# GpSimd's factors behind attention's last sums, the fifth product bank by bank, and residual additions on GpSimd

## The chip, the cores and the metric

The kernel runs on one core of a Trainium2 chip. The metric is the device time of one launch in microseconds (us). The kernel before took 3298.68 us in the median of three runs (3296.69 to 3300.23).

## What is computed

Eight images, each of 512 channels by 1024 pixels in fp32, pass through two attention layers. Both layers have the same form and differ in their weights and in the size of the groups of the normalisation (8 and 32 groups):

```python
xn  = groupnorm(x) * gamma + beta                 # [512, 1024] per image
qkv = qkv_w @ xn + qkv_b                          # q, k, v: [512, 1024] each
# 8 heads of 64 channels
attn = softmax(q_h.T @ k_h / 8, axis=-1)          # [1024, 1024] per head
out_h = v_h @ attn.T
x = proj_w @ out + proj_b + x
```

## The kernel before, in words

**Units.** A unit is one image in one layer, and the 16 units run one after the other: 8 of layer 0, then 8 of layer 1. The order of the instructions on each engine is the order of the Python calls; there is no scheduler. What a later step waits for comes from semaphores that the framework places by tiles. Tile pools give a buffer to a new tile when its last user has done with it. The pool that matters here, `ppool`, has five buffers of 128x1024. It holds the exponentials `p`, the tiles `xa` and `xb` for factors, `oa` and `ob`, `u3_v`, and the residual tiles `res00`, `res01`, `res10`, `res11`.

**Fast products.** Every 512x512 by 512x1024 product is done with seven products of half size instead of eight (Strassen in Winograd's form), in the order 1, 6, 2, 7, 5, 4, 3 (`ORDER`). For V one such level is used, and for Q, K and the output projection two levels: each of the seven is again seven products of 128-row quarters (`Stream.product`, L421). The factors of the right-hand side are sums and differences of parts of `xn` (the normalised input) or `ao` (attention's result). `Right.mix` (L217) makes the outer ones on VectorE. `Right.quarter` makes the quarters: on GpSimd for `xn` (the lambda at L933 issues them), on VectorE for `ao` (L990). Three of a pair's four quarter steps need only the outer factors; the fourth overwrites its input in place, and must wait until TensorE has read it.

**Stages of a unit.** First come the value products (`make_values`, L398): seven of 16 matmul instructions, into three pairs of PSUM banks. Their results are taken out by ScalarE (L606, L621) and VectorE (L607, L625 for the sixth, L632 for the seventh). Then come Q and K (`make_pairs`), then the output projection of the unit before (`project`), then attention of this unit. `hook(sel, k)` runs further work behind product k of a stage; the lists are written out with `at(...)` in the main loop.

**A product of the stream** (`Stream.product`). The part products 1, 6 and 5 are summed one after the other in a spare half bank `one`. ScalarE copies (`seed`, L426) that running sum into the four quarters of the main pair of banks, where TensorE adds the other parts. A seed must wait until VectorE has read what stood in that bank two products earlier. The last two parts and the reading out (`tail`) of a product come behind the first part of the next one (`close`), so that the seeds are covered. The tail of the very last product comes behind the first scores of attention (`close()` in `scores`). One part product (7) goes out on its own as `late` (L438), and GpSimd adds it to the right half of the result (`add_late`, L458).

**Reading out.** In `sum_steps`, the running sums p1, u2 and u3 are made by VectorE (L466/L469, L478, L486). The fifth product is needed twice: `w` (L496) adds it to u2 over both banks, then L509 (Q, K) or L546 (output) adds it to a result over both banks.

**Residuals.** In `project`, `load` brings the four residual tiles from memory. `take` (L546) adds a product to a tile, `more` (L550, VectorE) adds a running sum, and `store` (L553) sends it to memory from SP's queue. The stores of res11, res10 and res01 come behind `more`.

**Attention.** 64 steps of scores (L703), exponential (ScalarE, L713) and products with V (L733). VectorE sums the exponentials (L750 for the first two of eight, then L752), which is the softmax's denominator. At the end of each eight steps come ScalarE's L758 and VectorE's L759 to take the result out, a transpose (L764) and a reduction (L772). `reciprocals` (L789 to L798) and `divide` (L812) follow later, for the last pair of heads in the next unit's value stage. TensorE runs the products two steps behind the scores at a unit's start.

**Weights.** The left-hand factors are mixed once per layer on VectorE (L1064 runs such steps), and stored in memory as images that later units load. `MAKE` says which unit's attention mixes which weights. In layer 0, V, Q and K are mixed in the first unit's value, Q and K stages, and the output weights in the first unit's attention.

Of the kernel before, what the change touches and what calls it, by code (L numbers as in the profile page):

```python
# [32 lines left out]
def fast_path(ctx, tc, x, qkv_wT, proj_wT, vecs, groups, out, flag):  # L33
# [5 lines left out]
    nc = tc.nc  # L39
# [4 lines left out]
    FD = 512  # L44
# [415 lines left out]
    def sum_steps(l, bias, name, early=None):  # L460
# [32 lines left out]

        def w(main, m):
            t = st["u2"]
            on("DVE", nc.vector.tensor_add(t, main, t), m, 0, 1)  # L496

        return st, p1, u2, u3, w

    def make_pairs(stream, w, sel, bias, left, early, hook):  # L500
# [13 lines left out]
        def fifth(main, m, late):  # L514
            wide(main, m)
            result(1, 1, "u3")(main, m, late)

# [14 lines left out]
    def project(stream, w, left, hook):  # L532
# [15 lines left out]

        def more(r, h, name):
            add(res[r, h], res[r, h], st[name])  # L550

# [11 lines left out]
        def fifth(main, m, late):  # L563
            wide(main, m)
            take(1, 1, main, m, late)

        def fourth(*args):
            take(1, 0, *args)
            more(1, 1, "u3")
            store(1, 1)  # L570

        def third(*args):
            take(0, 1, *args)
            more(1, 0, "u3")
            store(1, 0)
            more(0, 1, "u2")
            store(0, 1)
# [98 lines left out]

    def attention(w, close, at_step):
        u = w.u
# [5 lines left out]
        def scores(s):  # L684
# [16 lines left out]
            for j in range(2):  # L701
                for e in range(2):
# [6 lines left out]
                    )  # L709
            if s == 0:  # L710
                close()
            p = ppool.tile([P, 2, FD], F32, tag="p", name=f"p_{u}_{s}")
# [180 lines left out]
    }  # L893
    MAKE = {0: (0, "o"), 1: (1, "v"), 2: (1, "q"), 3: (1, "k"), 4: (1, "o")}

    old = None
    for u in range(2 * B):
# [36 lines left out]

        at("v", 1, make_rooms, partial(right.mix, 3), part_of((2, 3), 0, 1, 2))
        at("v", 6, part_of((5, 6), 0, 1, 2))
        at("v", 2, partial(right.mix, 2), part_of((1, 7), 0, 1, 2))
        at("v", 7, part_of((1, 7), 3), part_of((4,), 0, 1, 2))
        at("v", 5, part_of((5, 6), 3))
        at("v", 4, part_of((4,), 3))  # L940
# [5 lines left out]
        if u == 0:  # L946
# [24 lines left out]
            at("q", 4, partial(run, inner_k[2:3]))  # L971
            at("q", 3, partial(run, inner_k[3:]), partial(store_image, 0, "k", left_first_k))
        else:

# [3 lines left out]
            def o_rooms(first_rooms):  # L978
                if first_rooms:
                    ta, tb = (trpool.tile([P, 2, FD], F32, tag="tr", name=f"o{i}_{u}") for i in "ab")  # L980
                    oa = ppool.tile([P, 2, FD], F32, tag="p", name=f"oa_{u}")
                    rooms = {(1, 7): (*halves(ta), halves(tb)[0]), (5, 6): (halves(tb)[1], *halves(oa))}
                else:
                    ob = ppool.tile([P, 2, FD], F32, tag="p", name=f"ob_{u}")
                    rooms = {(2, 3): (*halves(ob), halves(xt[:, 0])[0]), (4,): singles(xt[:, 1])}
                for pair, room in rooms.items():
                    o_parts[pair] = ro.quarter(pair, room, nc.vector)
# [38 lines left out]
        if u:  # L1026
            product = project(stream, old, left_slots[1], hook)
            at("k", 4, partial(old.load_res, 0, 0))
            at("k", 3, partial(load_xn, ahead, 2), partial(old.load_res, 1, 1), partial(old.load_res, 1, 0))
            at("o", 1, partial(stats_of, 0, 1))  # L1030
            at("o", 2, partial(stats_of, 2))
            at("o", 7, partial(stats_of, 3, 4))
            at("o", 5, partial(old.load_res, 0, 1))
            at("o", 4, partial(stats_of, 5))
            at("o", 3, partial(stats_of, 6, 7))
        else:
            at("k", 3, partial(load_xn, ahead, 2))
# [52 lines left out]

        attention(w, stream.close, at_step)
        old = w
# [277 lines left out]
```

## Time and profile before

| | |
|---|---|
| median of 3 runs | 3298.68 us (3296.69 to 3300.23) |
| the profiled execution | 3297.93 us, span 3296.1 us |
| TensorE (PE) busy | 3221.7 us, 98% |
| weight loads (PEld) | 2083.2 us, 63% |
| VectorE (DVE) | 2900.7 us, 88% |
| ScalarE (ACT) | 1888.6 us, 57% |
| GpSimd (POOL) | 889.7 us, 27% |
| granted TensorE clock | 0.998 |
| one unit (1435.59 to 1638.33 us) | 202.74 us; TensorE busy 199.77, VectorE 180.78, GpSimd 56.40 |
| GpSimd's step of a 128x512 quarter | 1.27 us at the least, 2.0 to 2.2 us where VectorE works beside it |
| store of a residual tile, issue to landing | 2.7 us median |

A row of the timeline gives the start in the span, the duration, the engine, the source line, the instruction, the tiles written and read, and the number of merged instructions; in brackets is the idle time before it and what ended that. A row of waits gives the engine and line that waited, whom it waited for, the total, the number of times and the longest. `issue` means that the engine waited for nothing that the profile shows. TensorE's matmuls overlap each other, so its idle time is best read from the pitch between starts.

### The profile page before, as it was taken

Reading aid. Unit: us, or ns where it says so; the run is one execution under the profiler, and the core shown is the slowest. Engines: PE = TensorE matmul, PEld = TensorE weight load, DVE = VectorE, ACT = ScalarE, POOL = GpSimd, SP = SyncE. Lnnn points to the kernel's source line nnn. Section 1 sums busy time; section 2 is a strip of 40 time slices with the busy share of each in tenths; the row PEclk is TensorE's granted clock in tenths of the full one; section 3 lists DMA queues with packets and bytes.
Section 4 is the critical chain, followed back from the end, with each engine's and each line's share of the span. In section 5 each row is a group of like instructions: output and inputs, shape, how many; then the busy total and the mean of one; then the engine's idle time right before and its main releaser. Section 6 shows DMA issues by size and latency. Waiting matters only on the chain.

```text
span 3296.1 us, 59529 instructions
## 1 busy us (share of the span) xinstructions
PE 3221.7 (98%) x22998; PEld 2083.2 (63%) x22998; DVE 2900.7 (88%) x3298; ACT 1888.6 (57%) x3077; POOL 889.7 (27%) x559
## 2 busy tenths in 40 slices
PE   9999999999999999999999999999999999999999
PEld 7466584665856658566584765847657575675753
DVE  7998989889898898998989989898898988989887
ACT  3645746457464574646646466574655746557464
POOL 5033140330413304132140422404223042330510
PEclk9999999999999999999999999999999999999999
DMA  5234243442424324233142331423314233232321
GB/s 192 81 128 129 77 142 99 129 129 94 133 89 138 122 60 136 80 104 115 55 143 79 108 119 41 155 73 102 123 48 151 73 114 105 76 124 78 112 74 48
DMA packets 151343, 344.82 MB, mean 105 GB/s; under 512 B 27152, under 2 KB 40976, under 8 KB 151056
## 3 DMA queue, kind: packets, MB, share of 16 engines
q1 hardware_dynamic: 151056, 340.94, 32.5%
q8 instruction: 186, 3.05, 0.4%
q14 instruction: 101, 0.83, 0.1%
HBM read 282.29 MB, written 57.02 MB: 103 GB/s over the span
## 4 chain that ended last, share of the span: by engine, by line
PE 70%; DVE 21%; issue 5%; ACT 2%; DMA 1%; SPq 0%; POOL 0%; DVEq 0%; ACTq 0%
PE s L703 18%; PE a L733 17%; PE s L421 17%; PE a L421 12%; DVE acc L752 9%; PE s L398 2%; PE a L398 2%; DVE tr L764 2%; DVE acc L750 2%; DVE ao L759 1%; ACT p L713 1%; DMA lt<-red 1%; DVE red L772 1%; DVE tot L793 1%; PE a L703 1%
## 5 line engine op out<-in xcount | busy, mean ns | idle before, releaser
L713 ACT ACTIVATE p<-s 128x1024 f32<-128x1024 f32 x976 | 1000.3, 1025 | 528.1 <-PE s L703 446.5
L733 PE MATMUL a<-p,v 64*64 64x512 f32 x8192 | 1123.1, 590 | 8.6 <-ACT p L713 8.6
L703 PE MATMUL s<-q,k 64*64 64x512 f32 x7808 | 1083.4, 591 | 3.5 <-ACT a L426 2.6
L752 DVE TENSOR_TENSOR acc<-acc,p 128x1024 f32<-128x1024 f32 x768 | 995.6, 1296 | 55.0 <-ACT p L713 5.6
L733 PEld LDWEIGHTS a<-p,v 64*64 64x64 f32 x8192 | 410.2, 131 | 479.8 <-ACT p L713 336.8
L703 PEld LDWEIGHTS s<-q,k 64*64 64x64 f32 x7808 | 424.1, 133 | 392.1 <-issue 383.6
L426 ACT COPY a<-s 128x256 f32<-128x256 f32 x1308 | 463.3, 357 | 302.0 <-PE s L421 184.4
L933 POOL TENSOR_TENSOR xa<-xn 128x512 f32<-128x512 f32 x16 | 36.7, 2296 | 1150.8 <-PE s L703 987.8
L438 ACT COPY late<-s 128x256 f32<-128x256 f32 x327 | 121.8, 373 | 178.7 <-PE s L421 178.7
L819 ACT ACTIVATE ao<-ao,vec 128x512 f32<-128x512 f32 x128 | 88.3, 714 | 221.9 <-DVE ao L812 221.9
L398 PE MATMUL a<-w,xn 128*128 128x256 f32 x768 | 178.2, 381 | 0.0
L398 PEld LDWEIGHTS a<-w,xn 128*128 128x128 f32 x768 | 144.4, 190 | 31.7 <-issue 12.2
L764 DVE STREAM_TRANSPOSE tr<-acc 128x1024 f32<-128x1024 f32 x128 | 157.8, 1233 | 0.0
L772 DVE TENSOR_REDUCE red<-tr 128x32 f32<-128x1024 f32 x128 | 154.2, 1205 | 0.6
L750 DVE TENSOR_TENSOR acc<-p,p 128x1024 f32<-128x1024 f32 x128 | 152.4, 1190 | 1.0 <-ACT p L713 1.0
L421 PE MATMUL s<-k,w 128*128 128x256 f32 x492 | 146.3, 379 | 0.0
L421 PE MATMUL a<-xn,w 128*128 128x256 f32 x492 | 146.3, 379 | 0.0
L421 PE MATMUL s<-xn,w 128*128 128x256 f32 x492 | 146.3, 379 | 0.0
L421 PE MATMUL a<-xt,w 128*128 128x256 f32 x462 | 139.0, 382 | 0.0
L288 POOL TENSOR_TENSOR y<-var,half 128x4 f32<-128x4 f32 (+1 forms) x17 | 33.1, 1946 | 375.2 <-DVE var L286 375.2
L421 PE MATMUL s<-xt,w 128*128 128x256 f32 x432 | 128.5, 379 | 0.0
L458 POOL TENSOR_TENSOR res<-res,late 128x512 f32<-128x512 f32 x60 | 103.6, 1726 | 88.4 <-DVE res L546 88.4
(203 smaller groups left out, 4678.9 us busy)
## 6 DMA issues: line engine op xcount, KB each, us to landing
w<-iq SPq DMA_DIRECT2D x105, 448.0 KB, 3.5
w<-ik SPq DMA_DIRECT2D x105, 448.0 KB, 6.2
w<-io SPq DMA_DIRECT2D x105, 448.0 KB, 3.4
rb<-drec SPq DMA_DIRECT2D x128, 256.0 KB, 3.9
w<-iv SPq DMA_DIRECT2D x105, 256.0 KB, 2.9
xn<-mid SPq DMA_DIRECT2D x36, 512.0 KB, 3.8
xn<-x_dram SPq DMA_DIRECT2D x32, 512.0 KB, 4.2
res<-x_dram SPq DMA_DIRECT2D x32, 512.0 KB, 6.1
```

Source lines behind the costliest of these rows:

```text
L398: step()
L421: nc.tensor.matmul(dst, a[j], b[j], start=start, stop=j != 1, skip_group_check=True),
L426: n = nc.scalar.copy(dst, one)
L438: on("ACT", nc.scalar.copy(late, seventh), s, 1)
L458: return nc.gpsimd.tensor_add(cols, cols, twice(late))
L703: nc.tensor.matmul(bank[e * H : (e + 1) * H, j, :], w.k[pr][j * H : (j + 1) * H, t * P + e * H : t * P + (e + 1) * H], w.q[pr][j * H : (j ...
L713: exp = nc.scalar.activation(p, bank, AF.Exp, scale=SCALE)
L733: nc.tensor.matmul(banks[r][j * H : (j + 1) * H, :], w.v[rows, t, lo : lo + D], p[rows, j, :], start=(t == 0), stop=(t == NT - 1),)
L750: nc.vector.tensor_add(acc, state["first"], p)
L752: nc.vector.tensor_add(acc, acc, p)
L764: nc.vector.transpose(tr, state["acc"].pop(c))
L772: nc.vector.tensor_reduce(red[:, :, qh, :], state["tr"].rearrange("p j (f i) -> p j f i", i=BL), AX.X, ALU.add)
```

## The change

- **Order of GpSimd's factors.** Before, the quarters of the pair (2, 3) are requested behind the first value product, those of (5, 6) behind the second, and of (1, 7) behind the third. Pairs (2, 3) and (5, 6) need only data that is ready during attention. Now (1, 7) comes first, behind the second value product. It needs VectorE's last mix, which stands behind attention's last sums. (5, 6), (2, 3) and (4,) follow. GpSimd works in order, so nothing of it starts earlier.
- **The fifth product.** For Q, K and the output, L496 and the addition behind it are each split into one operation per bank, in the order bank 0, bank 0, bank 1, bank 1.
- **Residual additions.** `more` for res11 and res10 goes to GpSimd and stands in the fifth and the fourth product's step, with the stores. `more` for res01 stays on VectorE and moves ahead of the third product's result. The load of res01 moves from the fifth product (fifth in order) to the seventh (fourth in order).
- **The tail.** The last product's tail is issued ahead of attention's first scores.
- **Rooms.** The projection's pairs (1, 7) and (5, 6) exchange their buffers, so that a buffer of `ppool` comes free for res01 earlier.
- **First unit.** The output weights of layer 0 are loaded in the first unit's Q stage and mixed in its K stage; its attention mixes nothing.

```diff
--- before.py
+++ after.py
@@ -491,9 +491,9 @@
                 )
             add_late(t, late)
 
-        def w(main, m):
-            t = st["u2"]
-            on("DVE", nc.vector.tensor_add(t, main, t), m, 0, 1)
+        def w(main, m, i):
+            t = st["u2"][:, i, :]
+            on("DVE", nc.vector.tensor_add(t, main[:, i, :], t), m, i)
 
         return st, p1, u2, u3, w
 
@@ -512,8 +512,13 @@
             return finish
 
         def fifth(main, m, late):
-            wide(main, m)
-            result(1, 1, "u3")(main, m, late)
+            to = tiles[1][:, :, FD:]
+            for i in range(2):
+                wide(main, m, i)
+                w.last[sel].append(
+                    on("DVE", nc.vector.tensor_add(to[:, i, :], main[:, i, :], st["u3"][:, i, :]), m, i)
+                )
+            w.last[sel].append(add_late(to, late))
 
         steps = {
             1: p1, 6: u2, 2: result(0, 0, "p1"), 7: u3, 5: fifth, 4: result(1, 0, "u3"),
@@ -546,8 +551,8 @@
             on("DVE", add(res[r, h], main, res[r, h]), m, 0, 1)
             add_late(res[r, h], late)
 
-        def more(r, h, name):
-            add(res[r, h], res[r, h], st[name])
+        def more(r, h, name, engine=nc.vector):
+            engine.tensor_add(res[r, h], res[r, h], st[name])
 
         def store(r, h):
             nc.sync.dma_start(block_rows(dst, r, h), res[r, h])
@@ -561,19 +566,22 @@
             store(0, 0)
 
         def fifth(main, m, late):
-            wide(main, m)
-            take(1, 1, main, m, late)
+            t = res[1, 1]
+            for i in range(2):
+                wide(main, m, i)
+                on("DVE", add(t[:, i, :], main[:, i, :], t[:, i, :]), m, i)
+            add_late(t, late)
+            more(1, 1, "u3", nc.gpsimd)
+            store(1, 1)
 
         def fourth(*args):
             take(1, 0, *args)
-            more(1, 1, "u3")
-            store(1, 1)
+            more(1, 0, "u3", nc.gpsimd)
+            store(1, 0)
+            more(0, 1, "u2")
 
         def third(*args):
             take(0, 1, *args)
-            more(1, 0, "u3")
-            store(1, 0)
-            more(0, 1, "u2")
             store(0, 1)
 
         steps = {1: p1, 6: sixth, 2: second, 7: u3, 5: fifth, 4: fourth, 3: third}
@@ -674,7 +682,7 @@
 
 
 
-    def attention(w, close, at_step):
+    def attention(w, at_step):
         u = w.u
         n_chunks = CC * NH
         n_steps = n_chunks * NT
@@ -707,8 +715,6 @@
                         start=True,
                         stop=True,
                     )
-            if s == 0:
-                close()
             p = ppool.tile([P, 2, FD], F32, tag="p", name=f"p_{u}_{s}")
             exp = nc.scalar.activation(p, bank, AF.Exp, scale=SCALE)
             state["exp"].append(exp)
@@ -891,7 +897,7 @@
         "stats": (4, 5, 6, 7, 10, 11, 12, 13), "norm": (15, 20, 27, 30),
         "apply": (32, 33, 36, 38, 39, 41, 43, 44),
     }
-    MAKE = {0: (0, "o"), 1: (1, "v"), 2: (1, "q"), 3: (1, "k"), 4: (1, "o")}
+    MAKE = {1: (1, "v"), 2: (1, "q"), 3: (1, "k"), 4: (1, "o")}
 
     old = None
     for u in range(2 * B):
@@ -932,11 +938,11 @@
         def part_of(pair, *which):
             return lambda: [parts[pair][i]() for i in which]
 
-        at("v", 1, make_rooms, partial(right.mix, 3), part_of((2, 3), 0, 1, 2))
-        at("v", 6, part_of((5, 6), 0, 1, 2))
-        at("v", 2, partial(right.mix, 2), part_of((1, 7), 0, 1, 2))
-        at("v", 7, part_of((1, 7), 3), part_of((4,), 0, 1, 2))
-        at("v", 5, part_of((5, 6), 3))
+        at("v", 1, make_rooms, partial(right.mix, 3))
+        at("v", 6, part_of((1, 7), 0, 1, 2))
+        at("v", 2, partial(right.mix, 2), part_of((5, 6), 0, 1, 2))
+        at("v", 7, part_of((1, 7), 3), part_of((2, 3), 0, 1, 2))
+        at("v", 5, part_of((5, 6), 3), part_of((4,), 0, 1, 2))
         at("v", 4, part_of((4,), 3))
         at("v", 3, part_of((2, 3), 3))
 
@@ -970,6 +976,13 @@
             at("q", 7, partial(run, inner_k[1:2]))
             at("q", 4, partial(run, inner_k[2:3]))
             at("q", 3, partial(run, inner_k[3:]), partial(store_image, 0, "k", left_first_k))
+            outer_o, inner_o = mix_left(left_slots[0])
+            at("q", 6, partial(load_raw, 0, "o", left_slots[0]))
+            at("k", 6, partial(run, outer_o[:2]))
+            at("k", 2, partial(run, outer_o[2:]))
+            at("k", 7, partial(run, inner_o[:1]))
+            at("k", 4, partial(run, inner_o[1:2]))
+            at("k", 3, partial(run, inner_o[2:]), partial(store_image, 0, "o", left_slots[0]))
         else:
 
             reciprocals, divide, bias_last = old.finish
@@ -979,7 +992,7 @@
                 if first_rooms:
                     ta, tb = (trpool.tile([P, 2, FD], F32, tag="tr", name=f"o{i}_{u}") for i in "ab")
                     oa = ppool.tile([P, 2, FD], F32, tag="p", name=f"oa_{u}")
-                    rooms = {(1, 7): (*halves(ta), halves(tb)[0]), (5, 6): (halves(tb)[1], *halves(oa))}
+                    rooms = {(5, 6): (*halves(ta), halves(tb)[0]), (1, 7): (halves(tb)[1], *halves(oa))}
                 else:
                     ob = ppool.tile([P, 2, FD], F32, tag="p", name=f"ob_{u}")
                     rooms = {(2, 3): (*halves(ob), halves(xt[:, 0])[0]), (4,): singles(xt[:, 1])}
@@ -1029,8 +1042,7 @@
             at("k", 3, partial(load_xn, ahead, 2), partial(old.load_res, 1, 1), partial(old.load_res, 1, 0))
             at("o", 1, partial(stats_of, 0, 1))
             at("o", 2, partial(stats_of, 2))
-            at("o", 7, partial(stats_of, 3, 4))
-            at("o", 5, partial(old.load_res, 0, 1))
+            at("o", 7, partial(old.load_res, 0, 1), partial(stats_of, 3, 4))
             at("o", 4, partial(stats_of, 5))
             at("o", 3, partial(stats_of, 6, 7))
         else:
@@ -1088,7 +1100,8 @@
             elif s in (6 * NT + 2, 7 * NT + 3):
                 right.mix(s // NT - 6)
 
-        attention(w, stream.close, at_step)
+        stream.close()
+        attention(w, at_step)
         old = w
 
     both = const.tile([P, 1], F32, name="both")
```

## The prediction

> **What bounds the kernel now.** A unit is one image in one layer; 16 follow each other. I read first the busy shares, then TensorE's waits, then one unit in the timeline (value stage from 1436.05 us; the units from there to the last repeat it).
>
> ```profile
> PE 3221.7 (98%) x22998; PEld 2083.2 (63%) x22998; DVE 2900.7 (88%) x3298; ACT 1888.6 (57%) x3077; POOL 889.7 (27%) x559
> ```
>
> TensorE never rests long: a change that adds no matmul and removes none can win only its idle time, 3296.1 − 3221.7 = 74.4 us. The waits tell whose it is:
>
> ```profile
> PE s L398 <- DVE u_v L625: 35.0, 15, 4.5
> PE s L421 <- ACT a L426: 13.6, 16, 0.9
> PE a L733 <- ACT p L713: 8.6, 6, 2.6
> PE s L703 <- ACT a L426: 2.6, 16, 0.2
> ```
>
> The first is the value stage: its fourth product waits for VectorE to take the second out of the bank (L625). The timeline of all engines shows why VectorE is late there:
>
> ```profile
> 1431.09 2.13 POOL L933 TENSOR_TENSOR xa<-xn 128x512 f32<-128x512 f32 x1 [77.47 <-PE s L703]
> 1432.01 2.29 DVE L752 TENSOR_TENSOR acc<-acc,p 128x1024 f32<-128x1024 f32 x1
> ...
> 1436.45 6.70 DVE L752 TENSOR_TENSOR acc<-acc,p 128x1024 f32<-128x1024 f32 x3
> ...
> 1439.94 4.35 POOL L933 TENSOR_TENSOR k<-xt,k 128x512 f32<-128x512 f32 x2
> ...
> 1447.21 1.22 DVE L625 TENSOR_TENSOR u_v<-s,p_v 128x1024 f32<-128x1024 f32 x1
> ...
> 1448.48 3.72 PE L398 MATMUL s<-w,xn 128*128 128x256 f32 x16 [1.80 <-DVE u_v L625]
> ```
>
> Each of the last sums takes 2.2 to 2.3 us while GpSimd makes factors beside it, against 1.27 (2.54 for two) a little earlier; each GpSimd step takes 2.1 to 2.2 against 1.27 when alone. Each waits for the other in turn.
>
> The second wait is the fifth product of Q (K's is 0.1):
>
> ```profile
> 1479.56 1.21 DVE L496 TENSOR_TENSOR u_q<-a,u_q 128x1024 f32<-128x1024 f32 x1
> ...
> 1480.69 1.21 DVE L509 TENSOR_TENSOR q<-a,u_q 128x1024 f32<-128x1024 f32 x1
> 1481.98 0.63 ACT L426 COPY a<-s 128x256 f32<-128x256 f32 x2 [1.39 <-DVE q L509]
> ...
> 1482.39 0.30 PEld L421 LDWEIGHTS s<-xa,w 128*128 128x128 f32 x2 [1.29 <-ACT a L426]
> 1482.39 0.70 PE L421 MATMUL s<-xa,w 128*128 128x256 f32 x2 [0.89 <-ACT a L426]
> ```
>
> VectorE reads both banks of the pair twice; only then may ScalarE's seed enter the first bank. The third place is the change from the output projection to attention:
>
> ```profile
> 1530.55 2.18 POOL L458 TENSOR_TENSOR res<-res,late 128x512 f32<-128x512 f32 x1 [1.73 <-DVE res L546]
> 1531.63 2.75 SPq L553 DMA_DIRECT2D mid<-res  x2
> ...
> 1534.43 1.02 ACT L713 ACTIVATE p<-s 128x1024 f32<-128x1024 f32 x1 [2.03 <-DMA mid<-res]
> ```
>
> The fourth exponential of a unit takes the buffer of res10, so it waits for that tile's store, 2.8 us after L550 made it ready. TensorE has no wait here yet: its products of that step come at 1536.20, 0.75 us after the exponential's end.
>
> **What the Trainium skill says.** "SBUF — State Buffer", section "Who interferes with whom": a VectorE instruction with two SBUF inputs and a GpSimd one that reads SBUF exclude each other for the whole instruction, and who comes first decides; one with a PSUM operand goes free. The trace agrees: L812 begins at 1434.23, GpSimd's step ends at 1435.44, L812 at 1436.52; and L625 (PSUM) keeps its 1.22 beside GpSimd. "GPSIMD Engine Reference", section "Elementwise — side-by-side cycle accounting", gives 4497 ns for an add of 2048 columns, so an estimate near 2.3 us for 1024. The trace has 0.73 (256 columns) and 1.27 (512); carried on, 1.27 + 2 × 0.54 = 2.35. I use 2.35.
>
> **The change, part by part.** Times are of this unit, in the clock of the trace before.
>
> *GpSimd's factors.* (32.1 stands for 1432.1 us, and so on; from Q on, 81.0 for 1481.0 and 24.7 for 1524.7.) Six GpSimd steps that lay at 1431 to 1444 now follow VectorE's mix (L217), behind the last sums. VectorE then runs alone: L217 to 32.1, one sum to 33.3, L812 to 34.5, three sums to 38.4, L759 0.6, transpose 1.2, reduction 1.2, mix 1.2: 42.5 in place of 47.2. L625 now waits for its own product instead (its matmuls end near 43.4) and is done at 44.7; the fourth product needs the bank at 46.5. So the wait goes wholly: 1.97 us of TensorE's pitch (0.2155 a matmul instruction). The three units with 4.1 to 4.5 are 2.6 later on VectorE and should keep about 0.3 each. Sum: 35 us waited, plus 15 restart gaps of 0.1 to 0.2, less 1: **−36**.
> What becomes late: GpSimd starts at 42.7 with twelve steps of 1.27 and four of 0.73, 18.2 us, and meets about five long and five tiny two-SBUF operations of VectorE (5 × 1.1 + 1): end at 61 to 67. Q's first product needs its quarters at 59.8 (made first, by 47), its third the last one at about 68. No wait, with 1 us or more left. VectorE in its turn is blocked in the reciprocals, two mixes and L812: L632 would end near 53.6 where the sixth product wants the bank at 53.7, and L607 at 56.9 where the seventh wants it at 57.2. So the small 0.5 wait for L632 may stay: I give it nothing.
>
> *Fifth products bank by bank.* Two operations of 1.21 become four of 0.68, with a pitch of some 0.62: +0.3 us for VectorE, but the first bank is free after 1.3 in place of 2.4 us. Q: seed at 81.0 to 81.36 where the matmul wants it at 81.34; the second bank at 82.3, 0.1 late at worst. So 1.15 becomes 0.2: 16 × 0.95 = 15. K: its 0.2 goes, 16 × 0.19 = 3. **−18**. (The output's 0.2 is in the next sum.)
>
> *Tail and residuals.* The last product's tail is now ahead of the scores: its final part must wait some 0.2 for the seed that the scores used to cover, but the two gaps before (0.33 and three of 0.1 to 0.16) go. Then the stores. The fifth leaves VectorE at 24.7. GpSimd's queue is now: late half of res11 24.9 to 26.2; whole-tile addition to res11 (2.35) to 28.5; VectorE's addition to res01 arrives at 26.4, is blocked, runs to 29.6; late half of res10 to 30.75; addition to res10 to 33.1; VectorE's first sum, blocked, to 34.2; late half of res01 to 35.3. VectorE takes the last product at 30.2 to 31.4, so TensorE's first products start at 31.5 in place of 31.06. Store of res10 at 33.15, landed and free 2.8 later: exponential 35.95 to 36.97, products at 37.1 against 36.2 now. The built program gives res01's buffer to the fifth exponential in ten units: store at 35.35, exponential 38.15 to 39.2, products 39.3 against 37.92: +1.4. In the other five +0.9, but there the kernel now loses 1.3 to a sum (L750, the 1.17 waits of L733). 10 × 1.4 − 5 × 0.4 = **+12**. No earlier store has a later place on SP's queue; only the load of res01 moves forward, behind the fourth product's store (issued near 19.2, landing 3.6 later as now, 3.6 before its use).
>
> What is not known is who gets the port at 26.4: GpSimd leads by 0.15 us. If VectorE is first, GpSimd's chain shifts by 1.2, meets the first sum too, and the fourth exponential starts at 37.2, the fifth at 39.4: products 2.15 and 2.65 later: 10 × 2.65 + 5 × 0.85 = +30. At best (no meeting at all) the chain ends at 32, the gain of the tail stays, and the cost is about 0; at worst, every GpSimd step blocked once, see below.
>
> *First unit.* The output weights of layer 0 are mixed in K's stage instead of attention. There a pile of VectorE work (L1064 1.08 us beside the norm's eight operations) made TensorE wait 2.62 at 147.36; that goes. Eight mixing steps, some 7 us, enter a stage with room; up to 1 us lost. **−2**.
>
> Sum: −36 − 18 + 12 − 2 = −44 us. The profiled execution took 3297.93 (span 3296.1 and 1.8 around it) and the median of the runs is 3298.68, 0.75 above. 3298.7 − 44 = **3255**.
>
> **The rivals.** (a) The forecast: 3255, with 3247 to 3264 as its own range. (b) VectorE first at the port, or GpSimd's large addition dearer: +30 for +12: 3273. For it: the lead is only 0.15 us. Against: GpSimd's next step follows its last within 0.1 us wherever both are ready. (c) The new order of factors shifts the wait: VectorE, blocked in the reciprocals, keeps 0.7 to 1.2 us per unit of the value wait at L632 or L607, the margins above being 0.1 and 0.3; 15 × 1 = +15 on (a): 3270; with (b) 3288. (d) Slower: the stores. If each of GpSimd's five operations ahead of the last store is blocked for a whole VectorE operation (2.2 + 3.45 + 2.2 + 3.45 + 2.2), the fifth exponential starts near 41.3 and products come 4.5 us late, 67 in all and not 12: 3298.7 − 56 + 67 = 3310. It decides from 3.7 us per unit (56/15). Against: too few two-SBUF operations of VectorE lie in that stretch, two or three. That the change doesn't do what it says can't be: the built order shows GpSimd's steps behind the mix.
>
> **How the numbers follow.** (a) 45%, (b) 22%, (c) with or without (b) 20%, (d) and similar new stalls 9%, a cancelling mixture near no change 4%. A measurement of this kernel can tell about 0.2%, 6.6 us, from no change; below 3292 is faster. Faster 0.86, same 0.05, slower 0.09. Range 3244 to 3288: all of (a), (b) and most of (c) lie in it; the lower end takes the stores at no cost (−12 on (a)).
>
> **What would show it.** The row "L398 <- L625" gone or under 5 us; the last sums at 1.3; L421's waits for L426 near 2. ScalarE's waits for the DMA of res at every unit's start, L733's waits for L713 grown from 8.6 to some 20 to 35. Unit length, now 202.74, near 200.1. Wrong if L625 or L632 still ends TensorE's wait, if L421 waits for GpSimd's factors, or if the attention's start loses over 3 us.

## The result, and the profile after

| | before | after |
|---|---|---|
| median | 3298.47 us (4 runs, 3296.69 to 3300.23) | 3260.35 us (4 runs, 3258.34 to 3265.24) |
| ratio after / before | | 0.9887, 95% interval 0.9870 to 0.9904 |
| profiled execution, its span | 3297.93, 3296.1 | 3261.41, 3259.6 |
| one regular unit | 202.74 | 200.39 |

The change wins 38 us. The forecast was 3255, 44 us: the sum of the terms is 6 too high, but the terms themselves are off by more, in both directions.

The busy shares of the kernel after, engine by engine:

```profile
PE 3208.7 (98%) x22998; PEld 2087.4 (64%) x22998; DVE 2862.9 (88%) x3362; ACT 1890.5 (58%) x3077; POOL 910.9 (28%) x589
```

TensorE executes the same 22998 instructions, and its busy time fell by 13.0 us all the same; the idle time fell by 23.5. Its waits in the kernel after (columns as before: total, times, longest):

```profile
PE a L739 <- ACT p L719: 23.4, 27, 2.7
PE a L739 <- DVE res L551: 10.4, 14, 0.7
...
PE s L711 <- POOL k L458: 3.6, 1, 3.6
PE s L398 <- DVE u_v L640: 2.0, 3, 1.6
```

The value stage's 35.0 us (L398 for L625, now L633) are gone, and so are the 13.6 us of the fifth products (L421). In their place the products of attention (L739, before L733) wait 33.8 us instead of 8.6: for exponentials, and for VectorE's reading of the last output product (L551, before L546).

The value stage of unit 8 (its first matmul is at 1619.40), in the timeline of the kernel after:

```profile
1617.63 3.88 DVE L758 TENSOR_TENSOR acc<-acc,p 128x1024 f32<-128x1024 f32 x3
...
1624.43 1.21 DVE L217 TENSOR_TENSOR xn<-xn 128x1024 f32<-128x1024 f32 x1
1625.88 1.27 POOL L939 TENSOR_TENSOR k<-xn 128x512 f32<-128x512 f32 x1 [88.98 <-DVE xn L217]
...
1626.68 1.22 DVE L633 TENSOR_TENSOR u_v<-s,p_v 128x1024 f32<-128x1024 f32 x1 [1.03 <-PE s L398]
...
1629.87 3.62 PE L398 MATMUL s<-w,xn 128*128 128x256 f32 x16
```

Three sums now take 3.88 us instead of 6.70, GpSimd starts behind L217, and L633 waits for its own product. The fourth product's row has no wait in brackets.

The fifth product of Q in the same unit:

```profile
1660.46 0.68 DVE L496 TENSOR_TENSOR u_q<-a,u_q 128x512 f32<-128x512 f32 x1
1661.06 0.67 DVE L519 TENSOR_TENSOR q<-a,u_q 128x512 f32<-128x512 f32 x1
...
1661.66 0.67 DVE L496 TENSOR_TENSOR u_q<-a,u_q 128x512 f32<-128x512 f32 x1
1661.83 0.63 ACT L426 COPY a<-s 128x256 f32<-128x256 f32 x2 [0.32 <-DVE q L519]
```

ScalarE's seed enters the first bank 1.37 us after VectorE's first reading began; before it was 2.42 (1479.56 to 1481.98).

The end of the output projection and the start of attention in that unit:

```profile
1705.83 2.35 POOL L555 TENSOR_TENSOR res<-res,u_o 128x1024 f32<-128x1024 f32 x1
1706.08 3.17 DVE L555 TENSOR_TENSOR res<-res,u_o 128x1024 f32<-128x1024 f32 x1
...
1708.13 2.28 POOL L458 TENSOR_TENSOR res<-res,late 128x512 f32<-128x512 f32 x1
...
1709.78 1.20 DVE L551 TENSOR_TENSOR res<-a,res 128x1024 f32<-128x1024 f32 x1
1710.49 2.37 POOL L555 TENSOR_TENSOR res<-res,u_o 128x1024 f32<-128x1024 f32 x1
...
1711.20 1.09 PE L739 MATMUL a<-p,v 64*64 64x512 f32 x8 [0.74 <-DVE res L551]
...
1712.80 2.27 POOL L458 TENSOR_TENSOR res<-res,late 128x512 f32<-128x512 f32 x1
...
1715.65 1.03 ACT L719 ACTIVATE p<-s 128x1024 f32<-128x1024 f32 x1 [3.62 <-DMA mid<-res]
...
1717.88 1.02 ACT L719 ACTIVATE p<-s 128x1024 f32<-128x1024 f32 x1 [1.20 <-DMA mid<-res]
```

GpSimd is the first at the port (1705.83 against 1706.08), so VectorE's addition takes 3.17 us; the last product is read late, and the fourth and the fifth exponential wait for stores.

### The profile page after: what moved, and what is told of

Read it like the earlier page. It is cut to its first block, busy times and chain, and to the rows that moved or that the text cites. A ratio compares the mean times of both kernels' runs of the same rounds, so it can differ in the third digit from the quotient of the medians.

```text
span 3259.6 us, 59781 instructions
## 1 busy us (share of the span) xinstructions
PE 3208.7 (98%) x22998; PEld 2087.4 (64%) x22998; DVE 2862.9 (88%) x3362; ACT 1890.5 (58%) x3077; POOL 910.9 (28%) x589
## 4 chain that ended last, share of the span: by engine, by line
PE 89%; POOL 4%; DVE 3%; DMA 2%; ACT 1%; issue 1%; SPq 0%; ACTq 0%; DVEq 0%; POOLq 0%
PE a L739 25%; PE s L711 23%; PE s L421 17%; PE a L421 12%; PE a L398 6%; PE s L398 5%; POOL res L555 2%; POOL res L458 2%; DMA mid<-res 1%; DVE acc L758 1%; DMA out_dram<-res 1%; ACT p L719 1%; PE a L711 0%; PE s L664 0%; PE a L664 0%
## 5 line engine op out<-in xcount | busy, mean ns | idle before, releaser
L719 ACT ACTIVATE p<-s 128x1024 f32<-128x1024 f32 x976 | 997.2, 1024 | 560.6 <-PE s L711 457.0
L739 PE MATMUL a<-p,v 64*64 64x512 f32 x8192 | 1126.6, 590 | 33.8 <-ACT p L719 23.4
L758 DVE TENSOR_TENSOR acc<-acc,p 128x1024 f32<-128x1024 f32 x768 | 951.6, 1239 | 90.5 <-ACT p L719 45.5
L739 PEld LDWEIGHTS a<-p,v 64*64 64x64 f32 x8192 | 407.5, 131 | 516.7 <-ACT p L719 389.5
L426 ACT COPY a<-s 128x256 f32<-128x256 f32 x1308 | 465.5, 357 | 278.0 <-PE s L421 197.3
L939 POOL TENSOR_TENSOR k<-xn 128x512 f32<-128x512 f32 x16 | 20.3, 1270 | 1324.1 <-DVE xn L217 1324.1
L398 PE MATMUL a<-w,xn 128*128 128x256 f32 x768 | 178.1, 381 | 0.0
L756 DVE TENSOR_TENSOR acc<-p,p 128x1024 f32<-128x1024 f32 x128 | 162.9, 1272 | 4.2 <-ACT p L719 4.2
L398 PEld LDWEIGHTS a<-w,xn 128*128 128x128 f32 x768 | 144.5, 190 | 31.4 <-issue 12.2
L421 PE MATMUL s<-xn,w 128*128 128x256 f32 x492 | 146.5, 379 | 0.0
L421 PE MATMUL a<-xn,w 128*128 128x256 f32 x492 | 146.4, 379 | 0.0
L421 PE MATMUL s<-k,w 128*128 128x256 f32 x492 | 146.3, 379 | 0.0
L421 PE MATMUL a<-xt,w 128*128 128x256 f32 x462 | 137.5, 379 | 0.0
L765 DVE TENSOR_TENSOR ao<-a,tmp 128x512 f32<-128x512 f32 x128 | 88.1, 688 | 48.9 <-ACT tmp L764 47.8
L421 PE MATMUL s<-xt,w 128*128 128x256 f32 x432 | 128.5, 379 | 0.0
```

The source lines that it names most:

```text
L398: step()
L421: nc.tensor.matmul(dst, a[j], b[j], start=start, stop=j != 1, skip_group_check=True),
L426: n = nc.scalar.copy(dst, one)
L719: exp = nc.scalar.activation(p, bank, AF.Exp, scale=SCALE)
L739: nc.tensor.matmul(banks[r][j * H : (j + 1) * H, :], w.v[rows, t, lo : lo + D], p[rows, j, :], start=(t == 0), stop=(t == NT - 1),)
L756: nc.vector.tensor_add(acc, state["first"], p)
```

## The experiments

In what follows "value stage" is the time from a unit's first value product to its first attention product (it holds Q, K and the projection too), and "attention" the time from there to the next unit's first value product, both read from the starts of TensorE's matmuls. In a regular unit they are 95.01 and 107.74 in the kernel before, 91.75 and 108.65 after. All medians stand against the kernel before on the same chip. Units are counted from 0, so units 1 to 4 are the second to the fifth.

**1. Each part alone, on the kernel before.**

The order of GpSimd's factors alone:

```diff
-        at("v", 1, make_rooms, partial(right.mix, 3), part_of((2, 3), 0, 1, 2))
-        at("v", 6, part_of((5, 6), 0, 1, 2))
-        at("v", 2, partial(right.mix, 2), part_of((1, 7), 0, 1, 2))
-        at("v", 7, part_of((1, 7), 3), part_of((4,), 0, 1, 2))
-        at("v", 5, part_of((5, 6), 3))
+        at("v", 1, make_rooms, partial(right.mix, 3))
+        at("v", 6, part_of((1, 7), 0, 1, 2))
+        at("v", 2, partial(right.mix, 2), part_of((5, 6), 0, 1, 2))
+        at("v", 7, part_of((1, 7), 3), part_of((2, 3), 0, 1, 2))
+        at("v", 5, part_of((5, 6), 3), part_of((4,), 0, 1, 2))
```

Expected: 

> The kernel before with one edit: the order of GpSimd's factors, (1, 7) first and all behind VectorE's last mix. Theory (port): the exclusion of the two engines on the last sums is what made the value stage wait, so nearly all of that gain comes back with this edit alone: about 36 us, 3262, and no wait of the value products for L625 (35.0 us before). Rival (relief): the value stage is late because VectorE has too much work in all, and only the operations taken from it help; then this edit, which takes none away, gives under 10 us, 3289 or more.

Measured: 3250.69 us, ratio 0.9857 (0.9840 to 0.9873), −47 us where −36 was forecast; the rival of relief, under 10 us, is out. TensorE's waits for L398 in this kernel:

```profile
PE s L398 <- DVE u_v L632: 1.6, 3, 0.8
...
PE s L398 <- DVE u_v L625: 0.2, 1, 0.2
```

The fifth products bank by bank alone:

```diff
-        def w(main, m):
-            t = st["u2"]
-            on("DVE", nc.vector.tensor_add(t, main, t), m, 0, 1)
+        def w(main, m, i):
+            t = st["u2"][:, i, :]
+            on("DVE", nc.vector.tensor_add(t, main[:, i, :], t), m, i)
```

with the two `fifth` functions in their new form, but the residual additions left as they were. Expected: 

> The kernel before with one edit: the fifth products of Q, K and the output bank by bank. Theory: 18 us from Q and K and up to 3 from the output, so 3277 to 3281; the 13.6 us that L421 waits for L426 falls under 2. Rival (relief): four operations in place of two load VectorE by 0.3 us at each of 47 places, so the gain is eaten: 3295 or more.

Measured: 3277.10 us, ratio 0.9935 (0.9919 to 0.9952), −21 us. The row L421 for L426 is gone entirely, and the value stage of a regular unit is 1.46 us shorter (95.01 to 93.55).

The residual additions alone, with stores, load and rooms as in the change, and the tail still behind the first scores:

```diff
+            more(1, 1, "u3", nc.gpsimd)
+            store(1, 1)
 
         def fourth(*args):
             take(1, 0, *args)
-            more(1, 1, "u3")
-            store(1, 1)
+            more(1, 0, "u3", nc.gpsimd)
+            store(1, 0)
+            more(0, 1, "u2")
 
         def third(*args):
             take(0, 1, *args)
-            more(1, 0, "u3")
-            store(1, 0)
-            more(0, 1, "u2")
             store(0, 1)
```

Expected: 

> The kernel before with one edit: two residual additions on GpSimd, their stores earlier in the program, the load of res01 earlier and the exchange of rooms that serves it; the tail stays behind the scores. Theory (stores): GpSimd's chain of late half, addition, late half, addition frees the exponentials' buffers 1 to 3 us later than VectorE did, so 12 to 40 us slower: 3310 to 3338. Rival (relief): two VectorE operations less per unit give time back, 3290 or less.

Measured: 3325.93 us, ratio 1.0087 (1.0070 to 1.0104), 28 us slower. The waits of attention's products for exponentials in this kernel, which were 8.6 us, 6 times:

```profile
PE a L733 <- ACT p L713: 24.4, 28, 2.6
PE a L733 <- DVE res L546: 2.6, 14, 0.2
```

So two parts win more than the whole change does (47 + 21 = 68 against 38), and the third is a loss.

**2. The residual part undone in the kernel after.** All four residual additions, their stores, the load and the rooms are as before; order, banks, tail and first unit are as in the change.

```diff
-            more(1, 1, "u3", nc.gpsimd)
-            store(1, 1)
 
         def fourth(*args):
             take(1, 0, *args)
-            more(1, 0, "u3", nc.gpsimd)
-            store(1, 0)
-            more(0, 1, "u2")
+            more(1, 1, "u3")
+            store(1, 1)
 
         def third(*args):
             take(0, 1, *args)
+            more(1, 0, "u3")
+            store(1, 0)
+            more(0, 1, "u2")
             store(0, 1)
```

Expected: 

> The changed kernel with the residual additions, their stores, the load and the rooms as in the kernel before; order, banks, tail and first unit as changed. Theory (stores): the waits of the products for the exponentials (23.4 us) and for VectorE (10.4) go mostly, so about 20 us faster than the changed kernel: 3235 to 3248. Rival (relief): slower than the changed kernel, 3262 to 3275.

Measured: 3220.12 us, ratio 0.9765 (0.9749 to 0.9781), faster than either theory had it. The 33.8 us for which attention's products waited are nearly gone:

```profile
PE s L711 <- POOL k L458: 3.6, 1, 3.6
PE a L739 <- ACT p L719: 2.5, 5, 0.5
```

The residual part as a whole (additions, stores, load and rooms, which were not tested one by one) costs 40 us inside this change. VectorE has room for the additions: TensorE's value products wait 1.1 us in all for its L640, 2.0 in the kernel after.

The same kernel with the tail of the last product put back behind the first scores:

```diff
-        stream.close()
-        attention(w, at_step)
+        attention(w, stream.close, at_step)
```

(and in `attention` the call of `close()` behind the first scores). Expected: 

> The kernel e4_vector_resid with the last product's tail behind the first scores again. Theory: the tail ahead of the scores saves some 0.3 us in each of 15 units and costs 2.4 in the first one, where the scores then wait for all of K; so 1 to 4 us slower than e4's 3220: 3220 to 3225. Rival (cover): the scores covered a seed, so putting them back saves time: under 3216.

Measured: 3224.88 us, ratio 0.9777 (0.9764 to 0.9790). The tail ahead of the scores is worth some 4.8 us. The two intervals overlap, the runs do not (3218.88 to 3222.20 against 3223.04 to 3225.79). A regular unit wins 0.4 (198.86 to 198.46); the first unit loses 3.1 (181.05 to 184.16).

**3. Where the residual part loses.** One suspicion was the order on SP's queue. In units 1 to 4 the raw weights of layer 1 are loaded (L166) at the start of attention. SP's queue and the waiting exponentials in unit 1 of the kernel after:

```profile
292.17 0.37 SPq L558 DMA_DIRECT2D mid<-res  x1
292.58 3.18 SPq L166 DMA_DIRECT2D w<-qkv_wT_dram  x4
295.86 0.41 SPq L558 DMA_DIRECT2D mid<-res  x1
302.41 1.02 ACT L719 ACTIVATE p<-a 128x1024 f32<-128x1024 f32 x1 [4.41 <-DMA mid<-res]
303.58 2.01 PE L739 MATMUL a<-p,v 64*64 64x512 f32 x16 [2.69 <-ACT p L719]
```

The store of res10 waits for GpSimd until 292.17, the loads queue behind it, and the last store behind the loads: the exponential that needs its buffer starts 6.55 us after that store was issued. The kernel before, in the same place:

```profile
292.33 0.37 SPq L553 DMA_DIRECT2D mid<-res  x1
292.75 2.36 SPq L166 DMA_DIRECT2D w<-qkv_wT_dram  x4
296.25 2.76 SPq L553 DMA_DIRECT2D mid<-res  x2
```

There only the first of the last three stores (res11) stands ahead of the loads, which are issued 2.9 us before the unit's first attention product (295.67), not 2.1 after it (290.50). The experiment puts the tail, and so the last store, ahead of the loads:

```diff
+        stream.close()
         wproj = None
         if last:
...
-        stream.close()
         attention(w, at_step)
```

Expected: 

> The changed kernel with the last product's tail issued ahead of the loads of raw weights (units 1 to 4) and of the last projection (unit 15), so that SP's queue has the store of res01 before these loads. Theory (queue): in these five units attention's start lost 1.5 to 4.3 us more than in the other ten, because that store waits behind the loads and lands 6.2 to 6.6 us after its issue; so about 10 us faster than the changed kernel, 3248 to 3253, and no wait of the products for the exponentials over 1 us. Rival (weights' mixing): VectorE is late in these units; then no change, 3258 to 3262.

Measured: 3250.01 us, ratio 0.9852 (0.9837 to 0.9868), 10 us under the kernel after. Attention of those four units fell from 112.73, 111.05, 113.88 and 111.48 to 110.02, 109.70, 109.93 and 109.95; the regular units stayed at 108.65. The longest wait for an exponential is now 1.5 us, where none over 1 was expected:

```profile
PE a L739 <- ACT p L719: 12.6, 29, 1.5
PE a L739 <- DVE res L551: 10.4, 14, 0.8
```

The second row, VectorE blocked by GpSimd, was tried next: VectorE's addition to res01 goes behind its reading of the last product.

```diff
             store(1, 0)
-            more(0, 1, "u2")
 
-        def third(*args):
-            take(0, 1, *args)
+        def third(main, m, late):
+            on("DVE", add(res[0, 1], main, res[0, 1]), m, 0, 1)
+            more(0, 1, "u2")
+            add_late(res[0, 1], late)
             store(0, 1)
```

Expected: 

> The changed kernel with VectorE's addition to res01 behind the last product's reading, so that it can't be blocked by GpSimd's large addition (3.17 us now) ahead of it. Theory (stores end it): the wait of the first products for L551 (0.74 in 14 units, 0.92 with its restart) goes, but the fourth and fifth exponential still wait for the same stores, so the time shifts there: 0 to 5 us faster, 3255 to 3261. Rival (block): the whole 14 us come back, 3246 to 3248.

Measured: 3251.19 us, ratio 0.9857 (0.9842 to 0.9872): 9 us faster than the kernel after. The row L739 for L551 is gone and a regular value stage is 0.92 shorter (91.75 to 90.83). But the wait for exponentials grew from 23.4 to 30.4:

```profile
PE a L740 <- ACT p L720: 30.4, 20, 2.3
```

Attention of a regular unit gave back 0.32 (108.97). Neither theory has this: the wait did not move to the exponentials whole, and the 14 us did not come back whole. Attention of units 1 to 4 was 114.14, 114.19, 113.14 and 112.20, but the profiled execution is the slowest of the four (3255.65; the others took 3250.68 to 3251.60). In its units 1, 2 and 3 the granted clock fell to 0.5 for 3.41 us behind the long wait, which costs about 1.7 us each time (half of 3.41), so these units are no fair measure of the edit.

Half the dose: GpSimd adds to res11 only, the addition to res10 is VectorE's again and both last stores stand behind the last product.

```diff
         def fourth(*args):
             take(1, 0, *args)
-            more(1, 0, "u3", nc.gpsimd)
-            store(1, 0)
-            more(0, 1, "u2")
 
         def third(*args):
             take(0, 1, *args)
+            more(1, 0, "u3")
+            store(1, 0)
+            more(0, 1, "u2")
             store(0, 1)
```

Expected: 

> The changed kernel with GpSimd adding to res11 alone; the addition to res10 and both last stores go back behind the last product, the one addition on VectorE. GpSimd then has two late halves and one addition of 2.35 us before the last store instead of two additions, and no store stands ahead of the raw-weight loads on SP's queue while it waits for GpSimd. If the loss of the residual part (40 us within the changed kernel) is the length of GpSimd's chain and the store that it holds up on SP's queue: 3218 to 3230, L739's waits for L719 under 6 us. If any addition of a whole tile on GpSimd costs its share, through the lock with VectorE: near 3240, half way between the kernels with both and with none.

Measured: 3236.40 us, ratio 0.9815 (0.9802 to 0.9829), 16 us above the kernel with none. That is two fifths of the 40 and near the second theory's 3240, but not for its reason. A regular value stage is 90.83, as with none, and a regular attention 107.98 against 107.64: a third of a microsecond per unit, not the half of the 1.9 that the whole residual part costs there (200.39 against 198.46). The rest is in other units: attention of units 1 to 5 is 110.40, 110.68, 112.63, 110.03 and 109.99, against 109.25, 109.00, 109.25, 108.90 and 107.64. In unit 3 of this kernel:

```profile
687.21 2.35 POOL L555 TENSOR_TENSOR res<-res,u_o 128x1024 f32<-128x1024 f32 x1
...
689.59 0.37 SPq L558 DMA_DIRECT2D mid<-res  x1
690.00 2.38 SPq L166 DMA_DIRECT2D w<-qkv_wT_dram  x4
...
693.14 1.50 SPq L558 DMA_DIRECT2D mid<-res  x2
...
699.57 1.09 PE L739 MATMUL a<-p,v 64*64 64x512 f32 x8 [2.58 <-ACT p L719]
```

The same loads and last stores in the kernel with none:

```profile
686.61 2.38 SPq L166 DMA_DIRECT2D w<-qkv_wT_dram  x4
...
689.09 2.75 SPq L558 DMA_DIRECT2D mid<-res  x2
```

With one addition, res11's store is the one that waits for GpSimd, and the loads wait behind it. So the expectation that no store would hold up the loads was wrong. Counted from the unit's first attention product (691.66 here, 689.14 with none), the loads come 0.9 us later and the last two stores 1.5 us later. Which of the two makes the exponentials late was not separated. Of unit 3's loss some 1.7 us is again a clock of 0.5 for 3.41 us behind the wait. Unit 5 loads no raw weights; there the fourth exponential waits for a sum of VectorE and not, as in unit 6, for a store:

```profile
1104.09 1.94 ACT L719 ACTIVATE p<-s 128x1024 f32<-128x1024 f32 x2 [4.57 <-DVE acc L758]
```

The regular units lose most of their time only with the second addition on GpSimd and the order that goes with it (198.8 us with one, 200.39 with two).

**4. Must the whole order change?** On the kernel before, only one of the two early pairs, (2, 3), is moved behind the mix; three steps of (5, 6) stay early.

```diff
-        at("v", 1, make_rooms, partial(right.mix, 3), part_of((2, 3), 0, 1, 2))
-        at("v", 6, part_of((5, 6), 0, 1, 2))
-        at("v", 2, partial(right.mix, 2), part_of((1, 7), 0, 1, 2))
-        at("v", 7, part_of((1, 7), 3), part_of((4,), 0, 1, 2))
-        at("v", 5, part_of((5, 6), 3))
+        at("v", 1, make_rooms, partial(right.mix, 3), part_of((5, 6), 0, 1, 2))
+        at("v", 6, part_of((1, 7), 0, 1, 2))
+        at("v", 2, partial(right.mix, 2))
+        at("v", 7, part_of((1, 7), 3), part_of((2, 3), 0, 1, 2))
+        at("v", 5, part_of((5, 6), 3), part_of((4,), 0, 1, 2))
```

Expected: 

> The kernel before with half of the order's edit: the three steps of (5, 6) stay ahead, beside attention's last sums, only those of (2, 3) move behind. Theory (port): VectorE is late by three blocked operations, 3.3 us, in place of six; it has 0.9 us to spare in the whole edit and the bank is wanted 1.8 us after that, so 0.5 to 1 us of wait for L625 stays in the ten regular units and up to 3 in the others: 12 to 20 us of the 47 are lost, 3263 to 3271. Rival (buffers): what helped was that xa and xb no longer take two of the exponentials' buffers during attention; then nothing is lost, 3251.

Measured: 3277.26 us, ratio 0.9939 (0.9925 to 0.9953), −21 us of the 47. The loss of 26 is more than the 12 to 20 expected, and the rival of the buffers, which loses nothing, is out. In this kernel's timeline the three steps still meet the last three sums, which take 6.71 us as before; the sum and L812 ahead of them are free of GpSimd and take 1.22 each, where they took 2.29:

```profile
1625.94 1.86 POOL L933 TENSOR_TENSOR k<-xt 128x512 f32<-128x512 f32 x1 [80.02 <-PE a L703]
...
1626.60 6.71 DVE L752 TENSOR_TENSOR acc<-acc,p 128x1024 f32<-128x1024 f32 x3
```

and the wait is partly found elsewhere, at L632:

```profile
PE s L398 <- DVE u_v L632: 14.1, 13, 1.1
...
PE s L398 <- DVE u_v L625: 7.9, 3, 3.2
```

What the order wins is that the two engines no longer meet, and three steps of GpSimd left beside the last sums keep more than half of it from being won (26 of 47).

**5. The best version.** All residual additions on VectorE; the tail ahead of the scores and of the weights' loads; in the first unit, where the scores would wait for K, the tail behind the first scores.

```diff
+        if u:
+            stream.close()
         wproj = None
         if last:
...
-        stream.close()
-        attention(w, at_step)
+        attention(w, stream.close, at_step)
```

(on the kernel of part 2, with `close()` behind the first scores in `attention`). Expected: 

> The changed kernel with all residual additions on VectorE, the tail of the last output product ahead of the scores in all units but the first, and there also ahead of the raw-weight loads on SP's queue; in the first unit behind the first scores. If the parts add: 3220 of the kernel with the additions on VectorE, less 2.4 in the first unit (the scores no longer wait 3.6 us for GpSimd's half of K), less about 1.4 in each of four units and 1 in the last from the stores ahead of the loads: 3211 to 3215. If the order on SP's queue only mattered because the store of res10 waited for GpSimd, the four units give nothing: 3217 to 3219.

Measured: 3214.40 us (5 runs, 3213.59 to 3214.72), ratio 0.9747 (0.9734 to 0.9761): 83 us under the kernel before, 46 under the change, and within the 3211 to 3215 expected if the parts add. Attention of units 1 to 4 is 108.13 in each (109.25, 109.00, 109.25 and 108.90 in the kernel of part 2). Its busy time, and what is left of the waits:

```profile
PE 3195.6 (100%) x22998; PEld 2033.3 (63%) x22998; DVE 2844.5 (89%) x3392; ACT 1891.6 (59%) x3077; POOL 829.0 (26%) x559
```

```profile
PE s L332 <- DMA xn<-x_dram: 4.5, 1, 4.5
PE s L711 <- POOL k L458: 1.9, 1, 1.9
```

## Why the prediction was right, and where its terms were not

The time was in the range, and the mechanisms were in the main those that the prediction named. That the sum came within 6 us is luck: three terms won 17 us more than forecast, and the fourth lost 23 more. By its own steps, with the single parts as measured:

| step | predicted | measured | from |
|---|---|---|---|
| order of the factors | −36 | −47 | part 1, alone on before |
| fifth products | −18 | −21 | part 1, alone on before |
| first unit | −2 | −5 | kernel with the tail back (−73.3) less the two above, if they add |
| tail and residuals | +12 | +35 | 40 for the residuals (part 2), −5 for the tail |
| sum | −44 | −38 | |

*Order.* Right in mechanism and in its times. The text had L217 end 6.45 us after the stage began, GpSimd start at 6.65 and L625 end at 8.65; in unit 8 it was 6.24, 6.48 and 8.50. Right too was "1.97 us of TensorE's pitch", but more came with it. In a regular unit the value stage fell by 2.45 us with the order alone. The starts of the matmul groups split it: 1.97 for the wait, 0.28 of the sixth product's wait for L632, and 0.20 in two groups whose second matmul began 0.1 late after a stop. The prediction gave the 0.28 nothing ("I give it nothing"), because it had VectorE blocked more than it was: L632 ended 15.35 us after the stage's start, not 17.55. In the eleven units with the short wait (1 and 6 to 15) the 0.28 and the 0.20 make some 5 of the 11 us.

The three units with long waits won 5.37, 5.33 and 4.57; the forecast let them keep some. It had no term for TensorE's clock. In the kernel before, unit 3's long wait ends so (the second row is that stretch alone: the eight matmuls in it were busy all of its 3.30 us, and the third figure from the end, 0.50, is the granted clock):

```profile
625.19 5.36 PE L398 MATMUL s<-w,xn 128*128 128x256 f32 x16 [4.45 <-DVE u_v L625]
625.20:628.50 3.30, 3.30 (x8) 2.67 (x9) 2.67 (x5) 0.00 (x0) 2.67 (x3) 0.50 0.03 7
```

The 16 matmuls take 5.36 us instead of 3.62. Units 3, 4 and 5 have one such stretch of 3.41 us each, up to 1.7 us lost in each; in the kernel with the order alone these units have none.

*Fifth products.* "So 1.15 becomes 0.2": the row is gone, nothing stays, and 16 × 0.2 is the size of the 3 us.

*Who is first at the port.* Right, and closely. Shifted by 179.65 (the fifth product leaves VectorE at 1704.35 in the trace after, at 1524.7 in the prediction's clock), the steps of the chain lie within 0.15 us of the forecast: the blocked addition ends at 1709.25 (1709.25), the last product is taken at 1709.78 to 1710.98 (1709.85 to 1711.05), and the exponentials start at 1715.65 and 1717.88 (1715.6 and 1717.8). A regular unit loses 200.39 − 198.85 = 1.54 us against the kernel without the residual part and with the tail back, where "+1.4" was forecast.

*The other units.* This step failed, the term "− 5 × 0.4". "No earlier store has a later place on SP's queue; only the load of res01 moves forward" looked at the residual tiles alone. The raw-weight loads of units 1 to 4, and the projection's weights in the last unit, stand on the same queue. The change puts a store that waits for GpSimd ahead of them, and the last store behind them. Against the kernel with the tail back, the units compare so: units 1 to 5 are 3.8, 2.1, 4.8, 3.7 and 1.3 us longer, 15.8 in all, and the last 3.8, where the prediction had −0.4 for a unit outside the ten. Putting the tail ahead of the loads gave 10 us back, so that much is shown to come from the queue's order, the 1.7 us of halved clock behind unit 3's wait of 2.37 included. The rest of the loss, 9.6 in six units, fits the 1.54 that regular units pay too. The prediction's own sign of being wrong, over 3 us lost at attention's start, came in units 1, 3 and the last: against the kernel before, attention is 3.2, 4.3 and 3.4 us longer there.

*First unit.* K's stage took the eight mixing steps; it didn't lose the 1 us. And the wait of 2.62 us that goes was worth more: a clock of 0.5 for 3.41 us followed it, and in the kernel with the tail back the first unit's attention is 4.4 us shorter than before (107.77 against 112.14). But the tail ahead of the scores, which the text had not followed into this unit, made the first scores wait for GpSimd's half of K:

```profile
83.56 2.04 POOL L458 TENSOR_TENSOR k<-k,late 128x512 f32<-128x512 f32 x1 [0.82 <-DVE k L509]
85.75 3.69 PE L711 MATMUL s<-q,k 64*64 64x512 f32 x16 [3.58 <-POOL k L458]
```

No output projection lies between K and the scores there. With the tail back behind the scores, the first attention product comes at 87.55 instead of 90.89.

*The rivals.* The shift of the wait to L632 or L607 did not come: L640 has 2.0 us in all. VectorE first at the port did not come. The losing case, stores at 67 us, named the right place: with +35 in all it got half of the way, but through the queue's order and the other units, not by blocked operations in every unit. "The last sums at 1.3", the row of L398 and L625 "gone or under 5 us" and the waits for the exponentials "some 20 to 35" (23.4) were borne out. Unit length "near 200.1" was 200.39.

*The bound.* That such a change "can win only its idle time", 74.4 us, is refuted: the best version won 83, and its span of 3210.7 is shorter than the 3221.7 us for which TensorE was busy before. With the order alone, idle time fell by 35.6 (74.4 to 38.8), just the predicted 36, and busy time by 11.2 more (3221.7 to 3210.5). Some 5 us of that are the halved clock that units 3 to 5 no longer have (3 × 1.7). In a regular unit the clock is 1.00 in both kernels, and busy time still fell from 199.78 to 199.24, some 5 us over units 6 to 14; that the modelled ends of matmuls next to a stop make this part fits the late groups above, but was not tested.

What stays open: which of the load and the rooms, if any, has a share in the loss of the residual part; how the loss of units 1 to 4 with one addition divides between the loads and the late last stores; why unit 5 of that kernel hands the fourth exponential a buffer that VectorE still reads; and how the gain of 9 us in the kernel without the block splits between its stages beyond the regular units.

## What to carry to other kernels

An operation moved to an idle engine takes the stores and loads with it that wait for it: list everything that stands on the DMA queue behind such a store, in every kind of unit, and not only the tiles of the change. Two engines that exclude each other are best kept apart in time: put the flexible one's work where the other reads PSUM or waits, and count the total of the two only where they meet. A row of waits on TensorE understates what its removal brings: here by a tenth of a microsecond per stop, by the small waits next to it, and by up to 1.7 us where the clock was halved behind a long one. The busy share is no floor.

## What the hardware showed that was not expected

- A residual store (2.7 us from issue to landing in the median of the kernel before) let its buffer go only 6.55 us after issue when four weight loads had been issued just ahead of it on the same queue (295.86 to 302.41). In the last unit, behind one load, it was 6.69 (3119.15 to 3125.84).
- GpSimd's addition of two SBUF tiles took 0.73, 1.27 and 2.35 us for 256, 512 and 1024 columns of 128 partitions. The prediction's estimate near 2.3 us for 1024, worked out from the Trainium skill's "GPSIMD Engine Reference", section "Elementwise — side-by-side cycle accounting" (4497 ns for 2048), agrees.
- TensorE's recorded busy time for the same 22998 instructions was 3221.7, 3208.7 and 3195.6 us in the kernels before, after and best. The granted clock was 0.5 for 3.41 us in units 0, 3, 4 and 5 before, for 3.41 us in unit 3 and 6.83 us in unit 0 after, and not at all in the best until its last 3 us.
- In the twelve kernels every stretch at 0.5, but for one at the very end of each execution, lies at a stop of TensorE of 2.0 us or more, or begins within 1.4 us of its end. Not every such stop has one: 2.69 us in unit 1 of the kernel after has none. The best version and the one with the tail back have no stop of 2 us behind the first load, and no such stretch.
